# Carrying the first layer's accumulation chain into the second layer of a Strassen feed-forward kernel

## The chip, the core and the metric

The kernel runs on one core of a Trainium2 chip. The metric is the device time of one execution in microseconds (us), as a median over executions. The engines named below are PE (TensorE: matmuls, and the loads of their weights), DVE (VectorE), ACT (ScalarE), POOL (GpSimd) and SP (SyncE, whose queue issues most of the DMAs of this kernel). Each engine works through its own instructions in program order.

## The reference, cut to what matters

For 4096 rows `x` of width 512: a modulated 512x512 product gives `xf`; then a shared expert and one of two routed experts, chosen per row by the sign of a score, are added to `x`:

```python
def _L0_ffn_ref(x, gate_w, w1, b1, w2, b2, sw1, sb1, sw2, sb2):
    top1 = jnp.argmax(softmax(xf @ gate_w.T), axis=-1)
    masked = xf[None, :, :] * one_hot(top1).T[:, :, None]
    h = relu(einsum('end,edh->enh', masked, w1) + b1[:, None, :])
    routing_output = (einsum('enh,ehd->end', h, w2) + b2[:, None, :]).sum(axis=0)
    shared = relu(xf @ sw1 + sb1) @ sw2 + sb2
    return routing_output + shared      # and x is added to it
```

All of it is float32: 512 in and out, 2048 hidden.

## The kernel before

The rows are worked in units of 1024. `z_unit` makes `xf` (four units, to about 123 us); then come four shared units (`s0` to `s3`), three large routed units (`r0` to `r2`) on rows sorted by expert, a routed unit of 512 rows (`r3`), and a rest of 256 rows; three pieces of 128 rows are hosted in the first layers of `r0` to `r2`. A unit is a first layer and a second layer, and each is a product of 2x2 blocks done by Strassen's scheme in Winograd's form: seven products in place of eight, with sums of blocks ahead of them and behind them.

In `layer2_twice`, which serves the four shared units and `r0` to `r2`, the scheme is used twice. The outer seven products are the calls of `seven`, in the order 1, 3, 2, 5, 7, 6, 4; they are called steps here. Inside a step there are seven products again, called P1 to P7. Each is eight matmul instructions of 128x256 (four chunks of float32, two instructions for each), by the names in the trace:

- P1 `a11`, P5 `S1`, P6 `S2`, P7 `S3`, P4 `a22`, P2 `a12`, P3 `S4`, in this order on PE
- U2 = P1 + P6, U3 = U2 + P7, and the four outputs `o22` = P5 + U3, `o21` = P4 + U3, `o11` = P1 + P2, `o12` = P5 + P3 + U2 (signs are in the prepared weights and operands)

Before the change P6, P7 and P4 each go to a PSUM bank of their own, and DVE adds what was before (L1299, L1302, L1306). P2 is accumulated into the bank of P1, and P3 into that of P5.

The operand sums of a step (`Operand.sums`, four tensor operations of 1024 elements, L821 to L824) and differences of hidden blocks (L1233) are handed out between the products of the step before, as its list `fill`; hooks under keys such as `("n", 4, 6)` (step 4, after its sixth product) do other units' work, for example the rows of the next unit that are gathered, transposed (`turn`, L1503) and copied.

A step's weights fill two tiles of the tag `w2`, of which there are three buffers. The first tile (call it W0) holds `a11` (256 KB, DMA at L1256) and the three sums S1, S2, S3 (768 KB, L1257). The second (W1) holds `a12` and `a22` (512 KB, L1261) and S4 (256 KB, L1264). All are issued on SP, at the start of the step in program order; SP runs ahead and waits for a free buffer. The hook `"m2"`, between steps 5 and 7, issues on SP the first weights of the next unit's first layer: 15 DMAs for a shared unit (L1449 to L1453), six for a large routed unit (L1598, L1599), eight for `r3` (L601 to L604).

The first layers: `layer1_once` for shared units and `r3`, and `layer1_twice` for `r0` to `r2`. The latter already keeps P1, P6, P7 and P4 of a step in one bank, with copies by ACT (L1021, L1036, L1040), and restores P1 into the bank by a copy (L1051) ahead of P2. P4, P3 and P2 of a step stand among the products of the next. Its fourteen steps end with ReLUs (L1071) on hidden blocks, four handed out behind each P7 (`give(relus, 4)`), and the sums for the first step of the second layer (`x1.sums`).

Of the kernel before, what the change touches and what calls it, by code (L numbers as in the profile page):

```python
# [9 lines left out]
F32 = mybir.dt.float32  # L10
# [6 lines left out]
def kernel(  # L17
# [35 lines left out]
    nc = tc.nc  # L53
    P = 128
# [5 lines left out]
    KD = D // P  # L60
# [404 lines left out]
        nc.vector.tensor_sub(t[:, 2], b22, b12)  # L465
        nc.vector.tensor_sub(t[:, 3], b21, t[:, 1])

    def load_z(u):
        for slot, k, t in ((B11, 0, 0), (B21, K2, 0), (B22, K2, T), (B12, 0, T)):
            nc.gpsimd.dma_start(zslot(slot), zTD[u][:, k : k + K2, t : t + T])  # L470

    lo, hi, t0, t1 = slice(0, K2), slice(K2, KD), slice(0, T), slice(T, U)
# [320 lines left out]
    def unit(name, W, src, bias, row, hooks, after):  # L793
# [31 lines left out]
                ]  # L825

        if split is not None:
            x1 = Operand(h11, (0, 1, 2, 3))
        def layer1_once():


# [114 lines left out]
        def layer1_twice():  # L946
# [39 lines left out]
            class Step:  # L986
# [70 lines left out]
                def end(self):  # L1057

                    g = self.g
                    relus.extend(later)  # L1060
                    later.clear()
                    done = {3: (h22, 1), 4: (h11, 0), 5: (h21, 1), 6: (h12, 0)}.get(self.j)
                    if self.j == 3:
                        for o, x in ((h12, h22), (h22, h21)):
                            for m in range(2):
                                at = slice(m * H4 + 2 * g, m * H4 + 2 * g + 2)
                                adds.append(lambda o=o[:, at], x=x[:, at]: plus(o, o, x))
                    if done:
                        h, half = done
                        for c in (2 * g, 2 * g + 1, H4 + 2 * g, H4 + 2 * g + 1):  # L1070
                            later.append(lambda c=c: nc.scalar.activation(  # L1071
                                h[:, c, :], h[:, c, :], AF.Relu,
                                bias=bias[:, c + half * H2 : c + half * H2 + 1], scale=1.0,
                            ))

            beside = [hooks.get(k, ()) for c in range(H2) for k in (("in", c), c)]
            state = [0, 0]
# [16 lines left out]
            for n, (j, g) in enumerate(steps):  # L1094
                if 2 < n + 2 < len(steps):
                    load(n + 2)
                step = Step(n, x)
                step.p1()
                step.p5()
                if before:  # L1100
                    before.p4()
                step.p6()
                give(adds, 2)
                if n == len(steps) - 1:
                    give(x1.sums, 1)
                more()
                if n == 0:
                    give(first_sums, 2)
                if n == len(steps) - 1:
                    before.p3()  # L1110
                    step.p7()
                    before.p2()
                else:
                    if before:
                        before.p3()
                        before.p2()
                    step.p7()
                give(wb_later, 1)
                give(relus, 4)
                give(adds, 2)  # L1120
                if n == 0:
                    give(first_sums, 2)
                else:
                    run_late(1)
                if g == 1:
                    x = x_next
                elif j < 6:
                    x_next = Operand1(j + 1)
                if before:
                    before.end()  # L1130
                if n == len(steps) - 2:
                    give(x1.sums, 2)
                more()
                before = step
            before.p4()
# [1 line left out]
            before.p2()  # L1137
            give(x1.sums, 1)
            before.end()
            give(relus + later, 12)  # L1140

        if split1:
            layer1_twice()
# [82 lines left out]
        def layer2_twice():  # L1226
# [21 lines left out]
                    for i in range(K2)  # L1248
                ]

            def seven(step, l, x, o, fill):

                a11, both, sums_of = parts(l)
                w = {}
                t = wpool.tile([P, H4, 4, P], F32, tag="w2", name=f"w2{name}_{step}_0")
                nc.sync.dma_start(t[:, :, 0], a11)  # L1256
                nc.sync.dma_start(t[:, :, 1:], sums_of[:, :, :3])  # L1257
                w.update({m: t[:, :, i] for i, m in enumerate(("a11", "S1", "S2", "S3"))})
                t = wpool.tile([P, 3 * H4 * P], F32, tag="w2", name=f"w2{name}_{step}_1")
                u = t[:, : 2 * H4 * P].rearrange("p (c d) -> p c d", d=2 * P)  # L1260
                nc.sync.dma_start(u, both)  # L1261
                w["a12"], w["a22"] = u[:, :, :P], u[:, :, P:]
                w["S4"] = t[:, 2 * H4 * P :].rearrange("p (c d) -> p c d", d=P)
                nc.sync.dma_start(w["S4"], sums_of[:, :, 3])  # L1264
                o11, o12, o21, o22 = (o[:, i, j * Q : (j + 1) * Q] for i in range(2) for j in range(2))
                fill, n = list(fill), 0

                def product(m, tag=None, ps=None):
                    start = ps is None
                    if start:  # L1270
                        ps = bank(tag, f"{m}{name}_{step}")[:, :Q]
                    for c in range(H4):
                        nc.tensor.matmul(  # L1273
                            ps, w[m][:, c, :], x.of[m][:, c, :],
                            start=(start and c == 0), stop=(c == H4 - 1), skip_group_check=not start,
                        )
                    return ps

                def more():
                    nonlocal n  # L1280
                    n += 1
                    upto = -(-len(fill) * n // 7)
                    for f in fill[len(done) : upto]:
                        f()
                        done.append(f)
                    at(("n", step, n))

                def temp(tag):
                    return work.tile([P, Q], F32, tag=tag, name=f"{tag}{name}_{step}", bufs=2)

                done = []
                s1, u2, u3 = temp("s1"), temp("u2"), temp("s1")
                p1 = product("a11", "po")
                nc.scalar.copy(s1, p1)  # L1294
                more()
                p5 = product("S1", "po")
                more()
                p6 = product("S2", "pa")
                nc.vector.tensor_add(u2, p6, s1)  # L1299
                more()  # L1300
                p7 = product("S3", "pa")
                nc.vector.tensor_add(u3, p7, u2)  # L1302
                nc.vector.tensor_add(o22, p5, u3)
                more()
                p4 = product("a22", "pa")
                nc.vector.tensor_add(o21, p4, u3)  # L1306
                more()
                product("a12", ps=p1)
                nc.scalar.copy(o11, p1)
                more()  # L1310
                product("S4", ps=p5)
                nc.vector.tensor_add(o12, p5, u2)
                more()

            at("m0")
            rlo, rhi = row[:, :K2], row[:, K2:]
            seven(1, "A11", x1, o21, x3.sums)
            seven(3, "S4", x3, o12, difference(h11, h12, h11) + x2.sums)
            seven(2, "A12", x2, o11, difference(h12, h22, h12) + x5.sums)
# [3 lines left out]
            seven(6, "S2", x6, c2, x4.sums + plus(o12, o22) + plus(o22, c1) + plus(o11, o21, rlo))  # L1323
            at("m3")
            seven(4, "A22", x4, c2, plus(o21, c2) + plus(o12, o21, rlo)
                  + plus(o22, o21, rhi) + plus(o21, c1))
            at("m4")
            for f in plus(o21, c2, rhi):
                f()
# [165 lines left out]
            in_offset=bass.IndirectOffsetOnAxis(ap=box["idx"][:, c : c + 1], axis=0),  # L1495
        )

    def turn(name, rows, to):

        for q in range(KD):  # L1500
# [5 lines left out]
    def prepare_unit(k):  # L1506
# [14 lines left out]
                gather(r, s0 // P + j)  # L1521
            box["rows"] = rows

        def half(t):
            rows = box["rows"][t * (W // P) : (t + 1) * (W // P)]
            turn(f"{k}_{t}", rows, lambda q: zslot(slots[q // K2, t], W)[:, q % K2, :])

        def first_sums():
            if n < U:
# [4 lines left out]

        return {
            "m0": [m0, lambda: box.update(b=begin(k))],
            ("n", 4, 1): [lambda: half(0)],
            ("n", 4, 3): [lambda: half(1)],
            ("n", 4, 6): [first_sums],
        }  # L1540

    def prepare_rows(k, key, tile_of, at0, at1):
# [9 lines left out]

        def second():
            zt, rows, _ = box[key]
            turn(f"{k}", rows, lambda q: zt[:, q, :n])

        return {at0: [first], at1: [second]}

# [71 lines left out]
    def next_small(k, at0=("n", 3, 1), at1=("n", 4, 5)):  # L1630
        return prepare_rows(k, "zp", zp_tile, at0, at1)

    box["ws"] = [(w, lambda: None) for w, _ in first]
    for u in range(NU):
# [9 lines left out]
            })  # L1644
        if u < NU - 1:
            hooks = merge(hooks, {
                ("n", 6, 7): [lambda: load_z(u + 1)],
                ("n", 4, 6): [lambda: z_sums()],
            })
        if u + 1 < NU:  # L1650
            hooks = merge(hooks, first_weights(lambda: shared_weights(u + 1)))
# [103 lines left out]
```

## Time and profile before

| | |
|---|---|
| three runs: median, lowest, highest | 1679.88, 1678.93, 1681.72 us |
| the profiled execution: its time | 1680.43 us |
| its span in the profile | 1678.7 us |
| granted TensorE clock | 0.998 |
| PE busy, first and last matmul | 1650.3 us; from 1.1 to 1670.4 us |
| DVE, ACT, POOL busy | 1159.9, 495.0, 190.4 us |
| second layers of the seven units with `layer2_twice` | 84.6 to 88.8 us each |
| first layers of `r0` to `r2` | 120.7 us each |

Every time in the profile counts from the span's start. A row of the timeline gives start, duration, engine, line of the kernel, operation, what is written and what is read, and how many instructions are merged; in brackets stands how long the engine was idle before it and what released it. Two letters at the end of a name tell the kind of unit: `w2s` is a `w2` tile of a shared unit, `w2r` of a routed one. A bank keeps the name of its first product, so P3 appears as `S1`, and P2 as `a11`.

### The profile page before, as it was taken

The numbers are of one execution on the slowest core, as the hardware profiler recorded it, in microseconds if no ns is written. First come the engines' busy times: TensorE is split into PE (matmuls) and PEld (weight loads), VectorE is DVE, ScalarE is ACT, GpSimd is POOL, SyncE is SP. The second block draws the span as 40 slices with busy tenths as digits, with TensorE's granted clock in tenths as the row PEclk, the third lists the DMA queues.
The fourth block names the chain that finished last, engine by engine and source line by source line (L and its number), as shares of the span: only waits on it lengthen the run. The fifth ranks groups of instructions, "written<-read, shape, count | busy, mean of one in ns | idle before, by whom it ended". The sixth has DMA issues, their size and how long they took to land. (4 is left out here: it accounts for less than half of the span.)

```text
span 1678.7 us, 19747 instructions
## 1 busy us (share of the span) xinstructions
PE 1650.3 (98%) x6786; PEld 1203.4 (72%) x6786; DVE 1159.9 (69%) x1949; ACT 495.0 (29%) x933; POOL 190.4 (11%) x252
## 2 busy tenths in 40 slices
PE   9999999999999999999999999999999999999998
PEld 4444478645884478644888878888788887888884
DVE  5676969776887859686875678756787567885310
ACT  2334420134003320134013471134711347114210
POOL 1221100010001000012000111012110121002210
PEclk9999999999999999999999999999999999999999
DMA  4768957698667947698655657556575565634661
GB/s 164 284 239 303 362 173 235 202 350 279 200 211 260 370 140 240 210 329 304 218 165 175 231 184 241 163 176 229 184 240 162 176 229 185 180 105 136 212 238 39
DMA packets 287370, 366.08 MB, mean 218 GB/s; under 512 B 18404, under 2 KB 218596, under 8 KB 287271
## 3 DMA queue, kind: packets, MB, share of 16 engines
q1 hardware_dynamic: 264240, 290.06, 52.9%
q0 software_dynamic: 21536, 73.16, 12.3%
q10 hardware_dynamic: 1494, 1.60, 0.3%
q8 instruction: 54, 0.88, 0.2%
q14 instruction: 46, 0.37, 0.1%
HBM read 265.92 MB, written 98.84 MB: 217 GB/s over the span
## 5 line engine op out<-in xcount | busy, mean ns | idle before, releaser
L847 PE MATMUL p1s<-zs_all,was 128*128 128x512 f32 x288 | 135.7, 596 | 2.5 <-ACT u2s L873 2.0
L847 PEld LDWEIGHTS p1s<-zs_all,was 128*128 128x128 f32 x288 | 52.9, 190 | 63.2 <-issue 56.2
L847 PE MATMUL p1s<-zs_all,wbs 128*128 128x512 f32 x192 | 89.2, 592 | 0.0
L1580 POOL DMA_INDIRECT out<-ar,idx x33 | 34.7, 1051 | 446.7 <-DVE ar L1579 426.9
L1005 PE MATMUL a11r<-tr,war 128*128 128x256 f32 x288 | 74.6, 381 | 3.3 <-ACT s1r L1021 3.0
L847 PEld LDWEIGHTS p1s<-zs_all,wbs 128*128 128x128 f32 x192 | 36.4, 190 | 46.0 <-issue 44.0
L1005 PEld LDWEIGHTS a11r<-tr,war 128*128 128x128 f32 x288 | 54.0, 190 | 13.1 <-ACT s1r L1021 4.2
L880 DVE TENSOR_TENSOR h1s<-p5s,u3s 128x512 f32<-128x512 f32 x32 | 22.0, 689 | 48.7 <-ACT u3s L877 37.5
L1273 PE MATMUL S1s<-zs_all,w2s 128*128 128x256 f32 x224 | 53.0, 379 | 0.5 <-ACT s1s L1294 0.5
L1574 POOL DMA_INDIRECT ar<-accD,idx x33 | 35.5, 1075 | 156.8 <-PE pst L1503 143.0
L1273 PE MATMUL a22s<-zs_all,w2s 128*128 128x256 f32 x224 | 52.9, 379 | 0.0
L1273 PE MATMUL S2s<-zs_all,w2s 128*128 128x256 f32 x224 | 52.9, 379 | 0.0
L892 DVE TENSOR_TENSOR h3s<-p5s,u2s 128x512 f32<-128x512 f32 x32 | 22.0, 687 | 42.9 <-PE p5s L847 42.9
L1005 PE MATMUL S1r<-zs_all,wbr 128*128 128x256 f32 x168 | 43.5, 381 | 4.2 <-DVE h3r L1015 4.2
L1273 PEld LDWEIGHTS S1s<-zs_all,w2s 128*128 128x128 f32 x224 | 42.4, 190 | 6.6 <-ACT s1s L1294 0.9
L1405 PEld LDWEIGHTS phr<-zp,ws 128*128 128x128 f32 x384 | 46.2, 192 | 0.9
L1405 PE MATMUL phr<-zp,ws 128*128 128x128 f32 x384 | 46.8, 275 | 0.0
L1273 PEld LDWEIGHTS a22s<-zs_all,w2s 128*128 128x128 f32 x224 | 42.6, 190 | 5.8
L1273 PEld LDWEIGHTS S2s<-zs_all,w2s 128*128 128x128 f32 x224 | 42.6, 190 | 5.8
L847 PE MATMUL p1s<-zs_all,wam 128*128 128x512 f32 x96 | 44.6, 595 | 1.2 <-ACT s1s L858 1.2
L470 POOL DMA_DIRECT2D zs_all<-zTD x16 | 11.5, 728 | 301.7 <-PE S1s L1273 220.6
L847 PE MATMUL p5s<-zs_all,wbs 128*128 128x512 f32 x96 | 45.2, 593 | 0.0
(482 smaller groups left out, 3909.6 us busy)
## 6 DMA issues: line engine op xcount, KB each, us to landing
ws<-w SPq DMA_DIRECT2D x48, 512.0 KB, 5.9
w2s<-w2S SPq DMA_DIRECT2D x28, 768.0 KB, 6.0
war<-w1E SPq DMA_DIRECT2D x42, 512.0 KB, 5.3
wbr<-w1E SPq DMA_DIRECT2D x42, 384.0 KB, 3.4
w2r<-w2E SPq DMA_DIRECT2D x21, 768.0 KB, 4.7
w2r<-s2E SPq DMA_DIRECT2D x20, 512.0 KB, 3.9
was<-s1S SPq DMA_DIRECT2D x24, 384.0 KB, 5.2
zTD<-zt POOLq DMA_DIRECT2D x8, 1024.0 KB, 5.2
```

Source lines behind the costliest of these rows:

```text
L470: nc.gpsimd.dma_start(zslot(slot), zTD[u][:, k : k + K2, t : t + T])
L847: nc.tensor.matmul(ps, self.w[l][:, k, :], zslot(zi, W)[:, k, :], start=(start and k == 0), stop=(k == K2 - 1), skip_group_check=not start,)
L880: nc.vector.tensor_add(h22[:, self.c, :], self.b5, self.u3)
L892: nc.vector.tensor_add(h12[:, self.c, :], self.b5, self.u2)
L1005: nc.tensor.matmul(halves_of(ps)[:, i], w[:, i, k % 4], self.x.of[m], start=(start and i == 0), stop=True, skip_group_check=True,)
L1273: nc.tensor.matmul(ps, w[m][:, c, :], x.of[m][:, c, :], start=(start and c == 0), stop=(c == H4 - 1), skip_group_check=not start,)
L1405: nc.tensor.matmul(ph[:, ts(i, P)], w[:, k * W + i * P : k * W + (i + 1) * P], zt[:, k, :], start=(k == 0), stop=(k == KD - 1),)
L1574: nc.gpsimd.indirect_dma_start(out=ar, out_offset=None, in_=accD[:, :], in_offset=at)
L1580: nc.gpsimd.indirect_dma_start(out=out[:, :], out_offset=at, in_=ar, in_offset=None)
```

## The change

- In `layer2_twice`, P6, P7 and P4 of every step but the first are accumulated into the bank of P1. ACT copies the partial sums out (U2, U3 and `o21`) and copies P1 back into the bank ahead of P2. Step 1 keeps separate banks and DVE adds.
- P4, P3 and P2 of a step are issued in the next step, behind its P1: the order on PE is P1, P4', P3', P2', P6, P5, P7 (a prime marks the step before). Step 1 has P1, P5, P6, P7; step 4, the last, has P1, P4', P6, P3', P2', P7, P5, P4, P3, P2.
- A step's weights are asked for behind the fourth product of the step before it, in program order, by `seven_weights`.
- `fill` lists are ordered anew, and hooks of step 4 are moved: transposes are spread over four places, `z_sums` over three, and the load of `B12` comes after the step's second product.
- In `layer1_twice`, ReLUs are handed out two at a time, behind P6 and behind P7; those of `h11` go to the front. `x1.sums` start two steps before the end.
- Transposes for small pieces (`prepare_rows`) share a bank, with one copy for it.

```diff
         if split is not None:
-            x1 = Operand(h11, (0, 1, 2, 3))
+            x1 = Operand(h11, (0, 1, 3, 2))
...
                     if done:
+                        now = [] if self.j == 4 else later
                         h, half = done
                         for c in (2 * g, 2 * g + 1, H4 + 2 * g, H4 + 2 * g + 1):
-                            later.append(lambda c=c: nc.scalar.activation(
+                            now.append(lambda c=c: nc.scalar.activation(
...
+                        if self.j == 4:
+                            relus[:0] = now
...
                 step.p6()
+                give(relus, 2)
                 give(adds, 2)
-                if n == len(steps) - 1:
-                    give(x1.sums, 1)
...
-                give(relus, 4)
+                give(relus, 2 if n < len(steps) - 1 else 0)
...
-                if n == len(steps) - 2:
-                    give(x1.sums, 2)
+                if n >= len(steps) - 3:
+                    give(x1.sums, {1: 2}.get(len(steps) - n, 1))
...
-            give(relus + later, 12)
+            give(relus + later, 16)
...
+                def next_sum(self, m, o, before):
+                    if self.chain:
+                        self.product(self.b1, m)
+                        nc.scalar.copy(o, self.b1)
+                    else:
+                        ps = bank("pa", f"{m}{name}_{self.step}")[:, :Q]
+                        self.product(ps, m, True)
+                        nc.vector.tensor_add(o, ps, before)
...
+                def p4(self):
+                    self.next_sum("a22", self.o21, self.u3)
+                    if self.chain:
+                        nc.scalar.copy(self.b1, self.s1)
...
+            before, asked = None, {1: seven_weights(1, "A11")}
+            following = {1: (3, "S4"), 3: (2, "A12"), 2: (5, "S1"), 5: (7, "S3"), 7: (6, "S2"), 6: (4, "A22")}
+
+            def seven(step, l, x, o, fill, from_=1):
+                nonlocal before
+                this = Seven(step, l, x, o)
+                if before is None:
+                    order = [this.p1, this.p5, this.p6, this.p7]
+                elif step == 4:
+                    order = [this.p1, before.p4, this.p6, before.p3, before.p2, this.p7, this.p5,
+                             this.p4, this.p3, this.p2]
+                else:
+                    order = [this.p1, before.p4, before.p3, before.p2, this.p6, this.p5, this.p7]
...
+                    if n == 4 and step in following:
+                        asked[following[step][0]] = seven_weights(*following[step])
                     at(("n", step, n))
...
             at("m2")
             seven(7, "S3", x7, c1, difference(h21, h21, h22) + x6.sums)
...
-            ("n", 4, 1): [lambda: half(0)],
-            ("n", 4, 3): [lambda: half(1)],
-            ("n", 4, 6): [first_sums],
+            ("n", 4, 1): [lambda: half(0, (0, 1))],
+            ("n", 4, 2): [lambda: half(0, (2, 3))],
+            ("n", 4, 4): [lambda: half(1, (0, 1))],
+            ("n", 4, 5): [lambda: half(1, (2, 3))],
+            ("n", 4, 6 if n == U else 8): [first_sums],
...
-                ("n", 6, 7): [lambda: load_z(u + 1)],
-                ("n", 4, 6): [lambda: z_sums()],
+                ("n", 6, 7): [lambda: load_z(u + 1, slice(0, 3))],
+                ("n", 4, 2): [lambda: load_z(u + 1, slice(3, 4))],
+                ("n", 4, 7): [lambda: box.update(z=z_sums(now=False)), lambda: box["z"].pop(0)()],
+                ("n", 4, 8): [lambda: box["z"].pop(0)()] * 2,
+                ("n", 4, 10): [lambda: box["z"].pop(0)()],
```

More of the change, by code (lines that the diff above doesn't have):

```diff
@@ L466, in quarter_sums, with load_z @@
         nc.vector.tensor_sub(t[:, 3], b21, t[:, 1])
-    def load_z(u):
-        for slot, k, t in ((B11, 0, 0), (B21, K2, 0), (B22, K2, T), (B12, 0, T)):
+    def load_z(u, which=slice(0, 4)):
+        for slot, k, t in ((B11, 0, 0), (B21, K2, 0), (B22, K2, T), (B12, 0, T))[which]:
             nc.gpsimd.dma_start(zslot(slot), zTD[u][:, k : k + K2, t : t + T])
@@ L1249, in plus, with seven_weights @@
                 ]
-            def seven(step, l, x, o, fill):
+            def seven_weights(step, l):
                 a11, both, sums_of = parts(l)
@@ L1264, in seven, with __init__, product @@
                 nc.sync.dma_start(w["S4"], sums_of[:, :, 3])
[L1265 to L1271, printed above, removed]
+                return w
+            class Seven:
+                def __init__(self, step, l, x, o):
+                    self.step, self.x = step, x
+                    self.w = asked.pop(step)
+                    self.o11, self.o12, self.o21, self.o22 = (
+                        o[:, i, j * Q : (j + 1) * Q] for i in range(2) for j in range(2)
+                    )
+                    self.chain = step != 1
+                    self.s1, self.u2 = (
+                        work.tile([P, Q], F32, tag=tag, name=f"{tag}{name}_{step}", bufs=2) for tag in ("s1", "u2")
+                    )
+                    self.u3 = work.tile([P, Q], F32, tag="u3q", name=f"u3{name}_{step}")
+                    self.b1 = bank("pa", f"a11{name}_{step}")[:, :Q]
+                def product(self, ps, m, start=False):
@@ L1272, in product @@
                     for c in range(H4):
                         nc.tensor.matmul(
-                            ps, w[m][:, c, :], x.of[m][:, c, :],
+                            ps, self.w[m][:, c, :], self.x.of[m][:, c, :],
                             start=(start and c == 0), stop=(c == H4 - 1), skip_group_check=not start,
                         )
[L1277 to L1285, printed above, removed]
-                    at(("n", step, n))
@@ L1288, in temp @@
[L1288 to L1313, printed above, removed]
+                def next_sum(self, m, o, before):
[6 more added lines that the diff above has]
+                        nc.vector.tensor_add(o, ps, before)
@@ new lines, in p1, with p5, p6, p7 @@
+                def p1(self):
+                    self.product(self.b1, "a11", True)
+                    nc.scalar.copy(self.s1, self.b1)
+                def p5(self):
+                    self.b5 = bank("po", f"S1{name}_{self.step}")[:, :Q]
+                    self.product(self.b5, "S1", True)
+                def p6(self):
+                    self.next_sum("S2", self.u2, self.s1)
+                def p7(self):
+                    self.next_sum("S3", self.u3, self.u2)
+                def c22(self):
+                    nc.vector.tensor_add(self.o22, self.b5, self.u3)
@@ new lines, in p4, with p3, p2 @@
+                def p4(self):
+                    self.next_sum("a22", self.o21, self.u3)
+                    if self.chain:
+                        nc.scalar.copy(self.b1, self.s1)
+                def p3(self):
+                    self.product(self.b5, "S4")
+                    nc.vector.tensor_add(self.o12, self.b5, self.u2)
+                def p2(self):
+                    self.product(self.b1, "a12")
+                    nc.scalar.copy(self.o11, self.b1)
+            before, asked = None, {1: seven_weights(1, "A11")}
@@ new lines, in layer2_twice @@
+            following = {1: (3, "S4"), 3: (2, "A12"), 2: (5, "S1"), 5: (7, "S3"), 7: (6, "S2"), 6: (4, "A22")}
[9 more added lines that the diff above has]
+                    order = [this.p1, before.p4, before.p3, before.p2, this.p6, this.p5, this.p7]
+                fill, done = list(fill), 0
+                slots = min(7, len(order)) - from_ + 1
+                for n, f in enumerate(order, 1):
+                    f()
+                    if n == (7 if before else 4):
+                        this.c22()
+                    upto = -(-len(fill) * max(0, n - from_ + 1) // slots)
+                    for g in fill[done:upto]:
+                        g()
+                    done = max(done, upto)
+                    if n == 4 and step in following:
+                        asked[following[step][0]] = seven_weights(*following[step])
+                    at(("n", step, n))
+                before = this
@@ L1317, in layer2_twice @@
             seven(1, "A11", x1, o21, x3.sums)
-            seven(3, "S4", x3, o12, difference(h11, h12, h11) + x2.sums)
-            seven(2, "A12", x2, o11, difference(h12, h22, h12) + x5.sums)
+            seven(3, "S4", x3, o12, x2.sums + difference(h11, h12, h11))
+            seven(2, "A12", x2, o11, x5.sums + difference(h12, h22, h12), 2)
             seven(5, "S1", x5, o22, difference(h22, h22, h11) + x7.sums)
@@ L1322, in layer2_twice @@
             seven(7, "S3", x7, c1, difference(h21, h21, h22) + x6.sums)
-            seven(6, "S2", x6, c2, x4.sums + plus(o12, o22) + plus(o22, c1) + plus(o11, o21, rlo))
+            seven(6, "S2", x6, c2, x4.sums + plus(o12, o22) + plus(o11, o21, rlo) + plus(o22, c1))
             at("m3")
             seven(4, "A22", x4, c2, plus(o21, c2) + plus(o12, o21, rlo)
-                  + plus(o22, o21, rhi) + plus(o21, c1))
+                  + plus(o22, o21, rhi) + plus(o21, c1), 5)
             at("m4")
@@ L1496, in gather, with turn @@
         )
-    def turn(name, rows, to):
-        for q in range(KD):
+    def turn(name, rows, to, which=None):
+        for q in range(KD) if which is None else which:
             pt = bank("pa", f"pst{name}_{q}")
@@ L1522, in m0, with half @@
             box["rows"] = rows
-        def half(t):
+        def half(t, which):
             rows = box["rows"][t * (W // P) : (t + 1) * (W // P)]
-            turn(f"{k}_{t}", rows, lambda q: zslot(slots[q // K2, t], W)[:, q % K2, :])
+            turn(f"{k}_{t}", rows, lambda q: zslot(slots[q // K2, t], W)[:, q % K2, :], which)
         def first_sums():
@@ L1554, in second @@
             zt, rows, _ = box[key]
-            turn(f"{k}", rows, lambda q: zt[:, q, :n])
+            per = T // n
+            for q0 in range(0, KD, per):
+                pt = bank("pa", f"pst{k}_{q0}")
+                for q in range(q0, q0 + per):
+                    for j, r in enumerate(rows):
+                        at = (q - q0) * n + j * P
+                        nc.tensor.transpose(pt[:, at : at + P], r[:, ts(q, P)], ident)
+                nc.scalar.copy(zt[:, q0 : q0 + per, :n], pt.rearrange("p (q n) -> p q n", n=n))
         return {at0: [first], at1: [second]}
@@ L1628, in next_routed, with next_small @@
         ))
-    def next_small(k, at0=("n", 3, 1), at1=("n", 4, 5)):
+    def next_small(k, at0=("n", 3, 1), at1=("n", 4, 8)):
         return prepare_rows(k, "zp", zp_tile, at0, at1)
```

## The prediction

> **What bounds the kernel now.** I read the page first: who is busy, and how much is idle.
>
> ```profile
> span 1678.7 us, 19747 instructions
> PE 1650.3 (98%) x6786; PEld 1203.4 (72%) x6786; DVE 1159.9 (69%) x1949; ACT 495.0 (29%) x933; POOL 190.4 (11%) x252
> ```
>
> PE is the bound; no product is added or removed, so only its waits can be won. Its idle time at both ends (1.1 us ahead of its first matmul, 8.3 us behind its last) is not touched. The waits of PE (total, times, longest, in us) show what is left:
>
> ```profile
> PE S1r L1005 <- DVE h3r L1015: 4.2, 3, 1.4
> PE a11r L1005 <- ACT s1r L1021: 3.0, 3, 1.0
> ...
> PE p5r L847 <- DVE wam L194: 1.4, 1, 1.4
> PE S1s L1273 <- DVE c0s L1303: 1.3, 1, 1.3
> ...
> PE S1s L1273 <- ACT s1s L1294: 0.5, 1, 0.5
> ```
>
> Matmul ends are modelled some 0.17 us late (a product of eight is shown as 1.89 us, but the next starts 1.73 us after it), so each wait costs about 0.17 us more than its idle time. The first two rows are in `layer1_twice`, the rest at places that the change moves. All together are below 15 us.
>
> Then the timeline of the second layers, PE and SP side by side, because weights are now asked for at other times. Unit `s0`, SP, from the end of step 2's P7:
>
> ```profile
> 255.57 0.36 SPq L1261 DMA_DIRECT2D w2s<-s2S  x1
> 255.97 0.51 SPq L1264 DMA_DIRECT2D w2s<-w2S  x1
> 256.53 0.51 SPq L1449 DMA_DIRECT2D was<-sw  x1
> ...
> 265.94 0.34 SPq L1453 DMA_DIRECT2D wbs<-s1S  x1
> 266.41 0.37 SPq L1256 DMA_DIRECT2D w2s<-s2S  x1
> 266.82 0.51 SPq L1257 DMA_DIRECT2D w2s<-w2S  x1
> ```
>
> This is W1 of step 5, the 15 DMAs of `"m2"`, then W0 of step 7. Between the first of them and L1256 lie 10.8 us, and that L1256, of 256 KB, took 4.5 us to land (the line of its issue, in a window of its own):
>
> ```profile
> DMA to landing us min/median/max: 4.5/4.5/4.5
> ```
>
> It took 2.7 to 3 us where nothing stood ahead of it. The DMA engines are full in this stretch (the last two columns are the DMA share and GB/s):
>
> ```profile
> 257.00:271.00 14.00, 14.00 (x67) 12.32 (x66) 13.02 (x16) 0.74 (x2) 0.00 (x0) 1.00 0.97 299
> ```
>
> In `s1` the same jam already reached PE: P1 of step 7 ran at 462.88, and its S1 waited for L1257, issued at 457.73, which landed 7.5 us later.
>
> ```profile
> 462.88 1.97 PE L1273 MATMUL a11s<-h3s,w2s 128*128 128x256 f32 x8
> 465.37 1.97 PE L1273 MATMUL S1s<-zs_all,w2s 128*128 128x256 f32 x8 [0.52 <-ACT s1s L1294]
> ```
>
> The releaser named is ACT, long done; 457.73 + 7.5 = 465.2 says DMA.
>
> **The change, part by part.**
>
> *Second layer, engines.* A chained step has 6 copies on ACT for 2, and 2 tensor operations on DVE for 5. DVE loses 3 x 0.42 us in 42 steps; it is not the bound, so alone this is worth nothing. ACT gains 4 x 0.37 us (the row L1294, 128x256) in a step of 12.1 us and has room. The new waits: P6, P7 and P4' each need a copy of the partial sum from the bank; 1.73 us of another product (5.2 us for P6) lie ahead of each, and a copy starts about 0.2 us behind the last matmul and takes 0.37. P2' needs two copies, out and back: 0.2 + 0.37 + 0.37 and some latency, about 1.0 us, beside the 1.73 us of P3'. P3' needs DVE's `o22`, 3.45 us ahead of it. I cost all at zero; the cover is 0.7 us for P2', and what is late beyond it is paid in 42 steps.
>
> *Second layer, old waits.* The wait at 284.46 in `s0` (pace lost: 1.6 us) was DVE, 1.3 us late with `o22` of step 7 behind small operations of the sort. `o22` now stands ahead of fewer DVE operations, and P3 a step later: gone. The one of 0.7 us in `s1` goes too, as W0 of step 7 is now asked for ahead of `"m2"`: -2.3 us.
>
> *First layers of r0 to r2.* Four ReLUs of 0.61 us each stood between the copies of U3 and of the next P1, so P6 of step 12 waited at 985.75; with two it is just in time: -1.2 us. At the end PE waited 1.6 us for DVE (1001.70), because three of the `x1.sums` (1.15 us each) stood ahead; one is left. By counting forward from 991.5, P3 still loses 0.5 us and P2 0.1 us to the restoring copy. With the short slow start behind each wait I get -2.6 us a unit, -7.8 us. In return 14 ReLUs for 12 stand ahead of the first copy of the second layer (1.2 us more): U2 and `o22` of step 1 end 0.15 us too late for P3: +0.5 us.
>
> *Step 4.* `z_sums` ahead of `r3` come earlier than the end by three products, so the sums of its weights (L194) are ready for P5: -1.4 us. The small pieces' transposes waited 0.3 us for a bank, three times; now they use one: -0.9 us. Moved loads and sums: `B12` is asked for 8.6 us ahead of the sum that uses it (5.5 us to landing); T1 and T2 end over 3 us ahead of their products. Zero; POOL waits longer, with nothing behind it that PE needs. On SP the small DMAs of `"m0"` now stand behind step 1's weights; what follows them, W0 of step 3, is prefetched some 10 us early: zero.
>
> *Weights.* Three buffers, and W1 of a step now lives until the fourth product of the next. So W0 of step n+1 takes the buffer of W1 of step n-1: free 6.9 us into step n, 5.2 us ahead of its P1. That covers 0.2 + 3 us of a free queue. Not behind `"m2"`: in SP's order stand W1 of step 7 (which waits for the end of step 5), the 15 DMAs, then W0 of step 6. This is the chain of the fence above moved from the end of step 2 to that of step 5; but there 17.3 us lay before P1 of step 7, here 12.1 us before P1 of step 6. And P1 leads its step on PE, so P4', P3' and P2', whose weights are there, queue behind it.
>
> From W1's issue to the landing of L1256 it was 15.3 (`s0`), 16.7 (`s1`), 15.1 (`s2`), 13.9 (`s3`), 13.3 (`r0`), 13.9 (`r1`), 9.3 us (`r2`, whose hook moves 1 MB). In `s1` 512 KB loaded by POOL at 443.69 were in the way, which now go earlier; I take 15.1. With 0.3 us for the two semaphores, less 12.1 us (12.9 in `s1`, where the sort's matmuls stand between): 3.5 + 2.5 + 3.3 + 2.1 + 1.5 + 2.1 = **+15.0 us**.
>
> Here the Trainium skill speaks otherwise: "DMA: Bandwidth & Descriptors", section "Anatomy of one DMA — SWDGE (gpsimd) path", gives a transfer about 2.0 us plus its bytes at 436 GB/s. W1, the hook and 256 KB are 3.8 MB: 10.7 us (an estimate by that page), in time, and no wait. It describes one transfer from another queue; the row here says 299 GB/s for this mix and 15.3 us. I take the row.
>
> Sum: -2.3 - 7.8 + 0.5 - 1.4 - 0.9 + 15.0 = +3.1 us. Not seen in the trace is which of the four `pa` banks P4 of step 1 gets: the one of P7 would wait 1.4 us in `r0` to `r2`, another none. I take none, 4.2 us as the upper end. Rounded up for this, +3.6 us: the profiled execution would go from 1680.4 to 1684.0; it was 0.5 us above the median, so 1683.5 us.
>
> **The rivals.**
>
> 1. *Transfers are in time: faster.* Place: P1 of step 6. If 3.8 MB land within 11.8 us of the end of step 5, all six waits vanish and -11.9 us stay: 1668. It decides at about 390 GB/s after 2 us of start and landing. For it: 343 GB/s in `r0` in 1036 to 1049. Against it: no stretch of the jam was that fast. If half of the waits remain, 1675.5.
>
> 2. *The copies back are late: slower still.* If P2' waits 0.3 us in each of 42 steps, 12.6 us: 1696. It decides where ACT is later than 0.7 us. For it: ACT's ReLUs and transposes' copies stand in the same queue. Against: the same restoring copy in `layer1_once` (L861) is in no wait of PE, and ACT was busy 7 of 87 us in a second layer.
>
> 3. *The change moves waits and no more: same.* The waits at step 6 are 12 us rather than 15, and won and lost cancel: 1680.
>
> **How the numbers follow.** Differences below 0.2%, 3.4 us, are about what a measurement of this kernel can't tell from none. My forecast (+1 to +8 us, the waits within 3 us of the sum, own range 1681 to 1688) has 0.55; the rival of equal size 0.18; faster 0.16; the copies' 0.11. The sum lies on the border of slower, and its unknown costs (the bank, small latencies) add rather than take; so of the forecast 0.45 lies above 0.2% and 0.10 within. Slower: 0.45 + 0.11 = 0.56, same 0.10 + 0.18 = 0.28, faster 0.16. The range from 1674 to 1691 leaves out most of rival 1's full case and the dear end of rival 2.
>
> **What would show it.** In the waits of PE of the changed kernel: `a11` at the line of the new `product`, six times, 1.3 to 3.4 us each, once in each of `s0` to `s3`, `r0`, `r1`, right behind the end of step 7, with L1256's DMA landing just ahead. In SP's timeline: the first weights' DMAs start at the end of step 5. Gone: `S1r <- DVE h3r` down to a third, `a11r <- ACT s1r`, `p5r <- DVE wam`, `S1s <- DVE c0s`. DVE falls by some 50 us, ACT rises by some 60. I am wrong if P1 of step 6 starts without a wait (then 1668), or if waits of P2 on ACT appear in most steps.

## The result, and the profile after

The changed kernel takes 1685.87 us (median of 8 runs, 1683.31 to 1693.76). The kernel before takes 1680.14 us in runs beside it (8 runs, 1678.91 to 1682.28). The ratio is 1.0041 with a 95% interval of 1.0028 to 1.0053, so the change costs 4.7 to 8.9 us, beyond the bound of 0.2% (3.4 us). The profiled execution is the shortest of the eight: 1683.31 us, 2.9 us above that of before, where the median is 5.7 us above.

The page of the changed kernel:

```profile
span 1681.5 us, 19753 instructions
PE 1649.2 (98%) x6786; PEld 1203.0 (72%) x6786; DVE 1109.7 (66%) x1823; ACT 558.5 (33%) x1090; POOL 188.1 (11%) x252
```

DVE has lost 50 us and ACT has gained 63.5 us, yet the end came no sooner: PE is still the bound, with the same 6786 instructions. What changed is where it waits. The waits of PE (total, times, longest):

```profile
PE a11s L1288 <- DMA w2s<-s2S: 7.9, 4, 2.3
PE a11r L1288 <- DMA w2r<-s2E: 4.0, 2, 2.1
...
PE S1r L1005 <- DVE h3r L1015: 1.0, 3, 0.3
```

The first two rows are new. They are six waits, one in each of `s0` to `s3`, `r0` and `r1`, and all lie at P1 of step 6. The other rows shown of before are down to a quarter (`S1r <- DVE h3r`, 4.2 us) or gone (`a11r <- ACT s1r`, `p5r <- DVE wam`, both of `S1s`).

SP's timeline in `s0`, from W1 of step 7 to W0 of step 6 (L1263, L1266 and L1258, L1259 are the old L1261, L1264 and L1256, L1257; L1496 to L1500 are the old L1449 to L1453):

```profile
267.42 0.36 SPq L1263 DMA_DIRECT2D w2s<-s2S  x1
267.82 0.51 SPq L1266 DMA_DIRECT2D w2s<-w2S  x1
268.37 0.51 SPq L1496 DMA_DIRECT2D was<-sw  x1
...
277.07 0.34 SPq L1500 DMA_DIRECT2D wbs<-s1S  x1
277.54 0.37 SPq L1258 DMA_DIRECT2D w2s<-s2S  x1
```

The chain of before, from the end of step 2, stands here at the end of step 5. W0 of step 6 is issued 10.1 us behind W1 of step 7, and 15 DMAs lie between. PE, at that place:

```profile
281.81 1.99 PE L1288 MATMUL a11s<-h1s,w2s 128*128 128x256 f32 x8 [2.34 <-DMA w2s<-s2S]
```

P1 stands first in its step, so P4', P3' and P2' of step 7, whose weights and operands are there, wait behind it. In `r0` the wait has a sequel:

```profile
1064.82 2.57 PE L1288 MATMUL a11r<-h1r,w2r 128*128 128x256 f32 x8 [1.89 <-DMA w2r<-s2E]
1067.17 3.05 PE L1288 MATMUL a11r<-zs_all,w2r 128*128 128x256 f32 x8
```

A product of eight takes 1.89 us elsewhere. Here the second takes 3.05 us, though it waits for nothing. The row by windows (its third column from the end is the granted clock) tells why:

```profile
1065.00:1070.00 5.00, 5.00 (x16) 4.11 (x16) 3.42 (x3) 0.37 (x1) 0.00 (x0) 0.66 0.56 173
```

PE is busy for all 5 us and the clock is 0.66 on average. The clock was at half for 3.41 us, from 1066.1 on. That costs 1.7 us and is in no row of the waits. The last section says when a wait has this sequel.

By stages, from the first product of each to that of the next, after less before: first layers of `r0` to `r2` -7.0 us; second layers +1.1 (`s0`), +0.6 (`s1`), +2.6 (`s2`), +2.0 (`s3`), +3.6 (`r0`), +2.1 (`r1`), -0.1 (`r2`); `r3` and the rest -1.7; the others within 0.7 each, -0.2 together. The sum is +2.9 us.

A wait costs more than its idle time: 0.17 us for the end of the product ahead, which is shown that much late, and 0.1 us for a slow start (the product behind the wait is shown with 1.99 us for 1.89). `s2`, where nothing else moved, shows it: 2.35 us idle, +2.6 us. The six waits so cost 13.4 us for 11.9 us of idle time.

### The profile page after: what moved, and what is told of

Read it like the earlier page. It is cut to its first block, busy times and chain, and to the rows that moved or that the text cites. A ratio compares the mean times of both kernels' runs of the same rounds, so it can differ in the third digit from the quotient of the medians.

```text
span 1681.5 us, 19753 instructions
## 1 busy us (share of the span) xinstructions
PE 1649.2 (98%) x6786; PEld 1203.0 (72%) x6786; DVE 1109.7 (66%) x1823; ACT 558.5 (33%) x1090; POOL 188.1 (11%) x252
## 5 line engine op out<-in xcount | busy, mean ns | idle before, releaser
L1288 PE MATMUL a11s<-zs_all,w2s 128*128 128x256 f32 x416 | 97.8, 379 | 0.0
L1288 PEld LDWEIGHTS a11s<-zs_all,w2s 128*128 128x128 f32 x416 | 78.9, 190 | 10.6
L1288 PE MATMUL a11r<-zs_all,w2r 128*128 128x256 f32 x312 | 74.9, 383 | 0.0
L1288 PEld LDWEIGHTS a11r<-zs_all,w2r 128*128 128x128 f32 x312 | 59.8, 193 | 8.2
L854 ACT ACTIVATE h2s<-p1s,b_sb 128x512 f32<-128x512 f32 x32 | 22.0, 687 | 77.9 <-PE p1s L847 77.9
L854 ACT ACTIVATE h0s<-p1s,b_sb 128x512 f32<-128x512 f32 x32 | 22.0, 687 | 73.5 <-PE p1s L847 73.1
L1288 PE MATMUL a11s<-h1s,w2s 128*128 128x256 f32 x160 | 38.2, 382 | 7.9 <-DMA w2s<-s2S 7.9
```

Of the source, the lines that this page charges most:

```text
L854: nc.scalar.activation(o, i, AF.Relu, bias=bias[:, hc : hc + 1], scale=1.0)
L1288: nc.tensor.matmul(ps, self.w[m][:, c, :], self.x.of[m][:, c, :], start=(start and c == 0), stop=(c == H4 - 1), skip_group_check=not start,)
```

## The experiments

The theory: the six waits are W0 of step 6 standing in SP's queue behind the first weights of `"m2"`. Rivals: the buffer of W0 comes free too late, whatever stands ahead; the chain on ACT itself costs time; the rest of the loss is not in the waits. Each kernel is the changed one with at most one edit, but for the last two: there it is the kernel before, and the kernel of the first experiment.

### The first weights asked for one step later

```diff
-        return {"m2": [do], "m4": [first_make]} if make else {"m2": [do]}
+        return {"m3": [do], "m4": [first_make]} if make else {"m3": [do]}
```

`"m3"` stands between steps 6 and 4.

> The changed kernel, with the hook that issues the first weights of the next unit moved from between steps 5 and 7 to between steps 6 and 4, so that on SP they stand behind the weights of step 4. Theory (the queue): all six waits at P1 of step 6 vanish, 12.8 us by the profile of the changed kernel, and nothing waits in their place; profiled span 1668 to 1670 (1681.5 before this edit), and with no wait of 2 us on PE the runs lie closer together: median 1669 to 1671. Rival A (the buffer: W0 of step 6 simply comes free too late, 5.2 us ahead of P1): the six waits stay, 1683 to 1687. Rival B (the transfers only move their jam): they meet the loads of the next unit's blocks at the end of the second layer, and the first products of the next first layer wait 2 to 4 us instead: 1680 to 1685.

Measured: 1668.22 us (1667.83 to 1671.14, 5 runs) against 1679.35 us before, ratio 0.9938 (0.9925 to 0.9952), a little less than expected. SP's timeline in `s0`, then the longest waits of PE:

```profile
267.04 0.36 SPq L1263 DMA_DIRECT2D w2s<-s2S  x1
267.44 0.51 SPq L1266 DMA_DIRECT2D w2s<-w2S  x1
273.94 0.36 SPq L1258 DMA_DIRECT2D w2s<-s2S  x1
274.34 0.51 SPq L1259 DMA_DIRECT2D w2s<-w2S  x1
```

```profile
PE a11r L1005 <- ACT u2r L1036: 2.0, 3, 0.7
PE p1s L847 <- ACT u2s L873: 2.0, 3, 0.7
```

W0 of step 6 now goes out as soon as its buffer is free, 6.9 us behind W1, as the prediction counted for a free queue. No wait of PE on a `w2` tile is left, and the one wait on a first-layer weight has not grown (0.4 us, 0.5 us before). By stages, the two profiles differ by 13.4 us at the six places and 1.7 us in `r0`, the clock's part; that is 15.1 of the 15.4 us between their spans. One key moves the time by 1% and gives a kernel that is faster than both. The buffer's coming free, at the same point in this kernel as in the changed one, is not late by itself.

### The first weights asked for in the middle of step 7

```diff
-        return {"m2": [do], "m4": [first_make]} if make else {"m2": [do]}
+        return {("n", 7, 4): [do], "m4": [first_make]} if make else {("n", 7, 4): [do]}
```

In this place they stand behind the weights of step 6 and ahead of W0 of step 4.

> The changed kernel, with the same hook put behind the fourth product of step 7, so that on SP the first weights stand behind W0 and W1 of step 6 and ahead of W0 of step 4. Theory (the queue): the six waits leave P1 of step 6 and appear at P1 of step 4, as long as before (1 to 2.6 us each, 11 to 14 us in all), since W0 of step 4 now stands behind the same transfers; span 1680 to 1683. Rival A (the buffer): waits at P1 of step 6 as in the changed kernel. If the jam were harmless wherever it stands: no waits, 1669.

Measured: 1692.26 us (1689.64 to 1695.3, 4 runs), ratio 1.0072 (1.0056 to 1.0087). The waits of PE:

```profile
PE a11s L1288 <- DMA w2s<-sw: 15.5, 4, 7.3
PE a11r L1288 <- DMA w2r<-w: 4.0, 2, 2.2
...
PE a11s L1288 <- DMA w2s<-w2S: 1.4, 1, 1.4
```

The source is now `sw` and `w`: weights of step 4, not of step 6. The waits have followed the hook by one step, which is what the theory asks for. The size was missed: 20.9 us of idle time, more than expected. The worst is `s0` with 7.3 us, and the clock was at half in three stretches in and behind such waits (6.83, 3.41 and 3.41 us).

### Fewer first weights at the hook

```diff
-            hooks = merge(hooks, first_weights(lambda: shared_weights(u + 1)))
+            hooks = merge(hooks, first_weights(lambda: shared_weights(u + 1), ((0,), (1,))))
```

Ten DMAs are issued at `"m2"` where a shared unit follows, and the last five later; `s3`, `r0` and `r1` keep what they had.

> The changed kernel, but for the shared units the hook between steps 5 and 7 loads two pairs of first weights in place of three (10 DMAs for 15, 0.9 MB less of 2.75); the third is loaded in the first layer, two pairs ahead of its use, as all later ones are. Theory (the queue): the jam in s0 to s2 is 3 us shorter (0.9 MB at 299 GB/s), more than their waits (2.3, 1.1 and 2.3 us of idle time), which vanish; those of s3, r0 and r1 stay at about 2 us each; median 1676 to 1680. Rival A (the buffer): the six waits stay as they are, 1684 to 1688.

Measured: 1677.93 us (1674.06 to 1682.86, 17 runs), ratio 0.9988 (0.9981 to 0.9995). The waits of PE:

```profile
PE a11r L1288 <- DMA w2r<-s2E: 3.3, 2, 2.0
...
PE a11s L1288 <- DMA w2s<-s2S: 2.2, 1, 2.2
```

The waits of `s0` to `s2` are gone (0.06 us is left in `s2`); the 2.2 us is that of `s3`, which the edit does not touch. The rival of the buffer falls: it is the same buffer, and it comes free at the same time. What stands ahead of the DMA in the queue sets when it lands.

### P1 of step 6 in third place

```diff
+                elif step == 6:
+                    order = [before.p4, before.p3, this.p1, before.p2, this.p6, this.p5, this.p7]
```

The queue is as in the changed kernel; only PE's order differs, and P4' and P3' give the weights 3.5 us more.

> The changed kernel, but in step 6 the order on PE is P4', P3', P1, P2', P6, P5, P7: its P1 comes two products (3.45 us) later, everything else as it was, the DMAs too. Theory (the wait is W0's late landing, counted against the place of P1): the six waits on DMA, all under 3.45 us, vanish in most runs; in their place P4' waits 0.6 to 0.7 us for ACT's copy of U3 in all seven units, since no other product lies between: 4.5 to 5 us; median 1672 to 1676. Rival A (something else holds PE at the step's start): the 2 us waits appear at P4' or P1 all the same, 1683 to 1688.

Measured: 1674.22 us (1673.31 to 1676.27, 7 runs), ratio 0.9965 (0.9954 to 0.9976). The waits of PE:

```profile
PE a11s L1288 <- ACT u3s L1297: 1.8, 4, 0.5
PE a11r L1288 <- ACT u3r L1297: 1.4, 3, 0.5
...
PE S1s L1288 <- DVE c0s L1318: 0.6, 1, 0.6
```

No wait on a DMA remains at step 6. The price is seen too: with P4' directly behind P7, the copy of U3 has no product to hide it, and PE loses 0.7 us in each of the seven units (by stages, beside the first experiment), 0.46 us of it idle. This is the uncovered cost of a copy by ACT, which the prediction set to zero with P1 as its cover. P3', a product earlier too, meets DVE's `o22` once, in `s0`.

### The clock alone: PE kept busy while it waits

```diff
+                if step == 6 and name in FILL:
+                    idle6 = bank("po", f"idle{name}")
+                    for _ in range(FILL[name]):
+                        nc.tensor.matmul(idle6[:, :P], ones, ones, start=True, stop=True)
```

`FILL` has 7 to 12 dummy matmuls (two instructions each) for each of the six units, about as long as the unit's wait. Their product is used nowhere.

> The changed kernel with matmuls of a constant tile into a spare bank (7 to 12 of them, 0.22 us each, 1.5 to 2.6 us in all at each place) ahead of P1 of step 6 in the six units that wait there; their results are not used. PE is then busy while it would have waited. Theory (the clock): the runs of the changed kernel lie above its profiled one because a wait of 2 us sometimes leaves PE on half its clock for a few us; with the waits filled the clock is granted as in the kernel before (0.998) in every run and the runs lie within 2 us of each other, median 1683 to 1685.5, span of the profile 1681 to 1683.5. Rival (the transfers land later in some runs): runs spread over 5 us or more as before, 1683 to 1694, whatever fills the wait.

Measured: 1684.75 us (1683.37 to 1687.75, 5 runs), ratio 1.0035 (1.0021 to 1.0048). The granted clock was 0.998 or 0.999 in every run, where seven of the changed kernel's eight runs had 0.995 to 0.997, and no stretch at half clock is in the trace ahead of the last matmul. So the waits do cause the stretches. But the time came down by about 1 us only, and the runs lie 4.4 us apart, where 2 us were expected. PE's timeline in `s0`:

```profile
279.39 2.84 PE L1344 MATMUL idles<-ones 128*128 128x128 f32 x24
284.05 1.99 PE L1289 MATMUL a11s<-h1s,w2s 128*128 128x256 f32 x8 [1.81 <-DMA w2s<-s2S]
```

Behind 2.8 us of dummies another 1.8 us of wait remains: L1258, issued at 278.12, landed 5.9 us later, where it took about 4.1 us in the profile of the changed kernel (an estimate from the start of P1). Between 262 and 288 us both traces hold the same 7537 packets and 6.44 MB, but not the same rate (last column, GB/s). First the changed kernel, then this one:

```profile
280.00:284.00 4.00, 2.19 (x10) 1.96 (x11) 4.00 (x5) 0.10 (x1) 0.00 (x0) 1.00 1.03 328
```

```profile
280.00:284.00 4.00, 2.23 (x21) 2.04 (x19) 4.00 (x5) 0.00 (x0) 0.00 (x0) 1.00 0.94 279
```

The fill also has a price of its own: the dummies hold PE for their whole length (1.7 to 2.8 us) even where the weights land sooner. By stages, PE loses 18.1 us at the six places of this profile, where the changed kernel's lost 15.1 us with the clock. Mixed, then: the clock's part is there, the landing at the end of a full queue differs from run to run by about as much, and the dummies take back some. Why the rate differs is left open.

### The changed kernel once more

No edit. It is to show whether the first profile is typical.

> The changed kernel once more, unedited, on the chip that runs the three others of this group, so that their differences are not one of chips. Theory (queue and clock): waits of PE on DMA at P1 of step 6 in six units, 11 to 14 us in all, and in most runs a granted clock of 0.995 to 0.997, lower than the 0.998 to 0.999 of the kernel before; median 1684 to 1688. If the spread came from one chip alone: clock 0.998 and more, all runs within 2 us.

Measured: 1687.87 us (1684.77 to 1690.23, 5 runs), ratio 1.0042 (1.0028 to 1.0055); the profiled execution, at 1690.23 us, is the longest of the five. Its waits of PE, and the row of `s0` by windows:

```profile
PE a11s L1288 <- DMA w2s<-s2S: 10.5, 4, 4.5
PE a11r L1288 <- DMA w2r<-s2E: 4.6, 2, 2.4
```

```profile
281.70:288.40 6.70, 4.92 (x12) 3.89 (x13) 4.88 (x5) 0.37 (x1) 0.00 (x0) 0.50 0.61 199
```

Of the 6.9 us between the two profiles' spans, the waits hold 3.2 (15.1 us for 11.9), and the clock about 4: it was at half for 6.83 us in `s0`, of which 4.9 us PE was busy, and for 3.41 us in each of `r0` and `r1`, 5.9 us lost for 1.7. The same six places, dearer.

### The first layers' edit alone

Before, with the edits of `layer1_twice` only (ReLUs two at a time, those of `h11` first, `x1.sums` from two steps before the end; diff above).

> The kernel before with the change's edits of layer1_twice alone: ReLUs two at a time, those of h11 first, and the sums for the second layer one step earlier. Theory (each part stands alone): first layers of r0 to r2 shorter by 2.3 us each, as between the two profiles, and nothing else: 7.0 us, span 1671.5 to 1672.5, median 1672.5 to 1674. Rival (the gain needs the second layer's new order, because the ReLUs left over delay its first copy): of the 7 us 2 to 4 come back as waits in step 1 of the second layer: 1675 to 1677.

Measured: 1671.68 us (1671.14 to 1672.22, 4 runs), ratio 0.9954 (0.9939 to 0.9969), some 1 us less than expected. `S1r <- DVE h3r` is down to 1.0 us as in the changed kernel, `a11r <- ACT s1r` is gone, and no wait is new at the start of the second layers. The 7.7 us between the medians (1679.35 less 1671.68) are the -7.0 us that the stages of the changed kernel show, within the spread; its own stages show -7.0 us there too. The first experiment's kernel, which has the rest of the change as well, is 3.5 us faster again (1668.22 for 1671.68). So of the 11.1 us that it gains on the kernel before, most are the first layers'.

### The chain taken out of the second layer

With the first weights at `"m3"` as in the first experiment, so that its time of 1668.22 us is the one to compare with:

```diff
-                    self.chain = step != 1
+                    self.chain = False
```

Every step uses separate banks and DVE's adds, in the new order.

> The kernel of e1 (first weights behind those of step 4) with the chain off in every step: P6, P7 and P4 in banks of their own with DVE's adds, as in step 1; the order of products stays. Theory (PE is the bound and only its waits count): within 1 us of e1, 1667.5 to 1669.5, while DVE is busy some 50 us more and ACT some 60 us less. Rival (DVE was close to being late, and the chain is what relieved it): waits of PE for DVE at P3 or P4 of many steps, 3 to 15 us: 1671 to 1683.

Measured: 1674.29 us (1673.57 to 1675.21, 5 runs), ratio 0.9967 (0.9953 to 0.998). A miss: the chain was expected to be worth next to nothing, and by the two ratios it is worth 0.0029, 4.9 us. By stages the second layers of `s0`, `s3`, `r0`, `r1` and `r2` are 0.9 to 1.4 us longer each, 5.3 us together; `s1` and `s2` lose nothing. Another 1.3 us is in the first layer of `s2`, where PE waits for a first-layer weight, outside the layers of the edit. In step 4 of `s3`, PE's timeline without the chain, then with it (first experiment):

```profile
864.30 1.99 PE L1288 MATMUL a22s<-zs_all,w2s 128*128 128x256 f32 x8 [0.24 <-ACT zs_all L1551]
866.14 1.34 PE L1550 MATMUL pst<-ident,rows 128*128 128x128 f32 x8
```

```profile
861.31 1.89 PE L1288 MATMUL a11s<-zs_all,w2s 128*128 128x256 f32 x8
863.04 1.04 PE L1550 MATMUL pst<-ident,rows 128*128 128x128 f32 x8
```

P4' stands behind ACT's copy of a transposed row: both want one of the four `pa` banks, which the chain leaves free. With the chain the same product, with the same operands, does not wait. This, the transposes behind it and the slow start behind each wait cost 1.0 us in each of `s3`, `r0` and `r1` and 1.1 us in `r2`; in `s0` DVE is late with `o22` again, 0.9 us. That names 5.0 of the 5.3 us. So the chain pays mostly in banks, and once in DVE's time; that it costs time itself, the second rival, falls.

## Why the prediction was right

It said slower, by waits at P1 of step 6 that outweigh the waits won. Both the sign and the mechanism held; point by point:

- *W0 of step 6 behind `"m2"`, +15.0 us.* Right in place, number and owner. The waits measured, as pace lost, 2.6, 1.3, 2.6, 2.4, 2.2 and 2.3 us, 13.4 us in all (16.7 in the second profile: 15.1 idle and six times 0.27). Putting `s1` at 2.5 us was the worst miss; `s0` was put at 3.5 and came at 2.6 and 4.8 us in the two profiles. The first and third experiments show the queue to be the cause. The choice of the row (15.3 us) over the page's formula (10.7 us) decided the sign: the formula's way is rival 1, and in the stretch on which it hangs the changed kernel's DMA ran at 275 GB/s, from 267 to 281 us, not at 390:

```profile
267.00:281.00 14.00, 12.47 (x58) 10.64 (x56) 12.59 (x32) 2.61 (x7) 0.00 (x0) 1.00 0.89 275
```

- *First layers of `r0` to `r2`, -7.8 us.* -7.0 us by stages; P3's wait was put at 0.5 us for each unit and is 0.3 us idle, with its 0.27 us as counted, so the small miss lies in the other terms. The edit alone gives -7.7 us.
- *Old waits of the second layer, -2.3 us.* -2.3 us: the stages of `s0` and `s1` in the first experiment, which has no new waits there (-1.56 and -0.76). But `s1` shows the same -0.76 us in the profile of the first layers' edit alone, whose second layer is the old one; that part came without the change too.
- *The late copy in step 1, +0.5 us.* Not there: no wait at P3 of step 1 is in the trace.
- *`r3`, -1.4 us, and the small pieces' bank, -0.9 us.* -1.7 us, and -0.9 us (0.35, 0.28 and 0.27 in the stages of `s3`, `r0` and `r1` of the first experiment).
- *P4 of step 1's bank, 0 to 4.2 us.* 0: no such wait.
- *All copies at zero.* Right in the order as it is, with P1 in front: no wait of P2' on ACT in 42 steps, and rival 2 is out. The order with P1 third shows what the cover is worth: 0.7 us a unit where it is gone.
- *DVE's relief is worth nothing.* Nearly right (0.9 us, once, in `s0`), but the chain's other effect, fewer banks in use, was not named. In the new order it avoids a loss of some 5 us, which the kernel before, with its other order, did not have; as the prediction took order and chain together, its sum is not touched.

That the profile came so near is in part luck: the waits were 1.6 us shorter than counted, and 1.7 us of half clock, which was not counted, took their place.

The step that failed is the last one, from the profiled execution to the median. The prediction added +3.6 us to both. The profile came 0.7 us under it (1683.3 for 1684.0), but the median 2.4 us over (1685.9 for 1683.5). Two things are missing from the sum. A wait on PE can halve the clock for 3.41 us afterwards, 1.7 us each time: once in the first profile, in three places in the second, 5.9 us together; by an estimate in the last section it costs 4.6 us in a usual execution. And the landing of the last DMA of a full queue varies by some 2 us between executions (4.1 and 5.9 us in two profiles), so that the kernel that hangs on it has a wide spread (5 to 10 us for the changed kernel, 3 us in the runs of the first experiment). How much of the 2.4 us is the landing's is not shown.

Rival 1's own arithmetic held well once its condition was made true: it gave 1668 us for transfers in time, and with the first weights one step later the kernel takes 1668.2.

## What to carry to other kernels

When a prefetch is moved, write down for each DMA its deadline and everything that stands ahead of it in its queue, with the rate that the trace shows for that mix: here a deadline of 12.1 us against a queue of 14.2 us (`s0`, 267.42 to 281.6) turned a gain of 12 us into a loss, and moving one hook behind it brought the gain back. Put the product with the latest weights behind those whose data are there, but count what its place in front was hiding. And where PE is the bound, add to a wait the half clock that can follow it, and compare medians and several profiles, not one.

## What the runs showed of the hardware

The half clock came after shorter waits than expected. The Trainium skill, "TensorE: Matmul & The Clock Gate", section "What's actually happening", has the clock drop after at least one idle window of about 3.4 us. Here 1.89 us were enough in `r0` of the changed kernel, 2.0 us in `r1` of the kernel with fewer first weights, while 2.34 us in `s0` of the changed kernel were not. The stretches, 3.41 us or, with waits of 4.5 and 7.3 us, 6.83 us, agree with the length that the page gives for a window.

What decides can be worked out from the traces. In each of the four that have stretches at half clock ahead of the last matmul, they start whole multiples of 3.413 us apart, those behind the last matmul included (in the second profile of the changed kernel 281.63, 1070.11, 1281.73 and 1684.51: 231, 62 and 118 of them). So the clock is set anew at fixed times 3.413 us apart. Two waits of the changed kernel's first profile, laid over these times (the third column from the end is again the clock):

```profile
277.62:281.03 3.41, 1.85 (x9) 1.29 (x7) 3.38 (x4) 0.37 (x1) 0.00 (x0) 1.00 1.05 320
281.03:284.44 3.41, 2.63 (x12) 2.35 (x13) 3.41 (x4) 0.37 (x1) 0.00 (x0) 1.00 1.02 344
1062.68:1066.10 3.42, 1.53 (x8) 1.16 (x7) 2.70 (x4) 0.37 (x1) 0.00 (x0) 1.00 1.08 355
1066.10:1069.51 3.41, 3.41 (x10) 2.71 (x9) 2.35 (x2) 0.37 (x1) 0.00 (x0) 0.50 0.47 138
```

The 2.34 us of `s0` are split between two windows, 1.56 and 0.78 us; the 1.89 us of `r0` lie in one, and the next runs at half clock. Over all ten traces, ahead of the last matmul, ten windows ran at half clock. Each followed one in which PE is shown idle for 1.86 us or more, and 1.81 us or less was never followed by one. (A window of 1.88 us that reaches past the last matmul, in the kernel without the chain, was not either, so the border is not sharp.) Where these times fall differs between executions (281.03 and 281.63 in the two profiles), so a wait of about 2 us costs 1.7 us more, or nothing, by chance. An estimate from these numbers: with the border at 1.85 us and the times at random, the six waits of the first profile meet 2.7 such windows in an execution, 4.6 us. That profile met one, and the median lies 2.6 us above it.
